# Moving digit work on VectorE behind the maxima: an attention and FFN layer on one Trainium2 core

## The chip, the cores and the metric

The kernel runs on one core of one Trainium2 chip. The metric is the device time of one execution in microseconds. Before the change it is 1046.27 us, the median of three runs (1044.57, 1046.27 and 1047.06).

## The reference

The input is `x` of shape (4, 512, 1024): four sequences of 512 tokens. The layer is causal attention with 16 heads of width 64, a residual with layer norm, then a linear layer with int8 weights, and again a residual with layer norm, all in fp32. Cut to what is computed:

```python
q, k, v = (x @ w.T for w in (w_q, w_k, w_v))          # (4, 512, 16 heads, 64)
q, k = rope(q), rope(k)                                # t * cos + rotate_every_two(t) * sin
scores = where(causal, q @ k^T, -1e9) / sqrt(64)
x = layernorm(x + (softmax(scores) @ v) @ w_out.T)
x = layernorm(x + x @ (weight * scales).T)
```

## The kernel before, in words

**Units and periods.** One unit is one sequence and one pair of heads, so there are 32 units `u`. Units 0 to 15 alternate between sequences 0 and 1, units 16 to 31 between sequences 2 and 3. The loop at L565 does one unit per turn, and one turn is called a period here. Period u holds the scores of unit u, its softmax, the product of probabilities and values of unit u-1 (`attend`, L477), and the projections of later units, which are cut into single matmuls (`tickets`) and drawn from a stream by `take(n)`. In period u the stream delivers products (u+1, 1), (u+1, 2) and (u+2, 0); the second number k is 0 for q, 1 for k and 2 for v.

**Digits.** An fp32 projection is made of three fp32r products. Every operand is held as a high digit h, a low digit l, and a combination d of both: `high_x` and `high_w` run on ScalarE, `low_x`, `diff_x`, `low_w` and `diff_w` on VectorE. `split_w` is `low_w` followed by `diff_w`. `product` (L265) first runs 16 matmuls on h and l into one PSUM buffer, which I call A(u,k), then 8 matmuls on d into a second, D(u,k). ScalarE copies A into `tA` (L292), and VectorE joins D and `tA` (L315). That last step, "the eviction", frees the buffer of D. The pool for these has two buffers, so D(u,k) cannot start before the D ahead of it is evicted.

**Softmax.** `scores` fills three PSUM tiles (groups 0, 1, 2) of a pool with three buffers. `maxima` on VectorE masks and reduces, `softmax` runs exponentials on ScalarE, reciprocals on VectorE and the scaling on GpSimd (L451). Then `transposes` turns the probabilities on VectorE (L456), sends them to DRAM (`turned`) and reads them back as `prT`. `attend` needs a buffer of the pool of score tiles, so it starts only when the exponentials of group 0 have been taken. `turn_values` (L470) turns the values v of a unit on VectorE, sends them to DRAM (`turned_v`) and reads them back as `va`, for `attend` one period later. The tile of v has one buffer (L250), so v of the next unit cannot be evicted before the copy to `turned_v` has read the last one.

**Order.** The order on PE, VectorE and ScalarE is the order of the Python calls. Work outside the loop's own order is hung up with `later(u, slot, f)` and done by `run(u, slot)`; the slots of a period are, in order: early, between, after, first, turn, mid, second, late, end. The order of the DMA issues on SyncE (SP) and of GpSimd's work comes out of the build. Each queue is in order: an instruction that waits holds all that are behind it.

**New sequences.** When unit u+2 belongs to another sequence, `new_sequence` (L321) loads its x in four parts of 512 KB through a ring of three `stage` buffers and hangs up the digit work of the parts. This occurs for u = 14 and 15 (sequences 2 and 3), and for u = 30 and 31, where the "sequences" are the two halves of `w_out` (B and B+1); u = 31 has a list of its own, which the change leaves alone. ScalarE's `high_w(0)` for the first rows of the output product is in slot early of period 30 and waits for a load named `sa`.

Of the kernel before, what the change touches and what calls it, by code (L numbers as in the profile page):

```python
# [38 lines left out]
def attention_ffn_kernel(  # L39
# [107 lines left out]
    def later(u, slot, f):  # L147
        plan.setdefault((u, slot), []).append(f)
# [8 lines left out]
    def load_x2(b, n, tile=None):  # L157


        t = staged[b, n] = stage(f"sx_{b}_{n}", [P, 2, S]) if tile is None else tile  # L160
        cs = slice(2 * n, 2 * n + 2)
        nc.sync.dma_start(out=t, in_=xT[b, :, cs, :] if b < B else wo[:, cs, ts(b - B, S)])
# [5 lines left out]
    def low_x(b, n):  # L168
        h, l, d = (t[:, 2 * n : 2 * n + 2, :] for t in XD[b % 2])
        nc.vector.tensor_tensor(l, staged.pop((b, n)), h, SUB)  # L170
# [5 lines left out]
    def load_w(k, hp):  # L176
        t = staged["w", k] = stage(f"sw_{k}_{hp}", [P, NC, P])
        nc.sync.dma_start(out=t, in_=(wq, wk, wv)[k][hp])

    def load_ao(t, tile=None):  # L180

        tile = staged["w", t % 3] = stage(f"sa_{t}", [P, NC, P]) if tile is None else tile
        nc.sync.dma_start(out=tile, in_=ao[t // NI][:, :, ts(t % NI, P)])
# [25 lines left out]
    def high_w(k):  # L209
        t = staged["w", k]  # L210
        nc.scalar.activation(WD[k][0], t, AF.Copy, scale=LESS)
        nc.scalar.activation(t, t, AF.Copy, scale=1.0 / X12)

    def low_w(k):
        h, l, d = WD[k]
        nc.vector.scalar_tensor_tensor(l, h, -1.0 / X12, staged.pop(("w", k)), op0=MUL, op1=ADD)  # L216

    def diff_w(k):
        h, l, d = WD[k]
        nc.vector.tensor_tensor(d, h, l, SUB)  # L220

    def split_w(k):
        low_w(k)
        diff_w(k)

    with tc.tile_pool(name="raw", bufs=2) as rawp, tc.tile_pool(name="qk", bufs=2) as qkp, ExitStack() as heads:
        def rope(u, k):

            raw, rot = prod.pop((u, k)), prod.pop(("rot", u, k))
            if u not in qk:  # L230
                qk[u] = qkp.tile([P, 2, S], FP, tag="qk", name=f"qk_{u}")
            nc.vector.tensor_mul(rot, rot, sin_sb[:, k, :])  # L232
            nc.vector.tensor_mul(raw, raw, cos_sb[:, k, :])
            out = qk[u][:, k, :]
            if k == 0:

                out = out.rearrange("p (i r s) -> p r i s", i=NI, r=R)
                raw, rot = (t.rearrange("p (r i s) -> p r i s", i=NI, r=R) for t in (raw, rot))
            nc.vector.tensor_add(out, raw, rot)  # L239

        def swap(u, k):

            raw = prod[u, k]
            rot = prod["rot", u, k] = rawp.tile([P, S], FP, tag="rot", name=f"rot_{u}_{k}", bufs=2)
            for p in range(2):
                nc.sync.dma_start(out=rot[p::2, :], in_=raw[1 - p :: 2, :])

        def raw_tile(u, k):
            tag = "v" if k == 2 else "raw"
            t = prod[u, k] = rawp.tile([P, S], FP, tag=tag, name=f"{tag}_{u}_{k}", bufs=1 if k == 2 else 2)  # L250
            return t
# [13 lines left out]
        def product(u, k, n):  # L265

            b, hp = units[u]
            w, r = WD[k], XD[b % 2]
            if n in (0, 2 * NC):
                prod["A" if n == 0 else "D"] = pjp.tile([P, S], FP, tag="pj", name=f"p_{u}_{k}_{n}")  # L270
            ps = prod["A" if n < 2 * NC else "D"]
            c, part = (n // 2, n % 2) if n < 2 * NC else (n - 2 * NC, 2)
            nc.tensor.matmul(  # L273
                ps,
                lhsT=w[part][:, c, :],
                rhs=r[part][:, c, :],
                start=n in (0, 2 * NC),
                stop=n in (2 * NC - 1, NT - 1),
            )
            last = u == NU - 1  # L280
            more = last or units[u + 1][1] != hp

            if more and n == 0:
                load_ao(k) if last else load_w(k, units[u + 1][1])

            b_next = units[u + 2][0] if u + 2 < NU else B + b % 2
            x_next = k == 2 and b_next != b
            if x_next and n == 0:
                new_sequence(u, b_next, True)
            if n == 2 * NC - 1:  # L290
                prod["tA"] = rawp.tile([P, S], FP, tag="tA", name=f"tA_{u}_{k}")
                nc.scalar.activation(prod["tA"], ps, AF.Copy, scale=1.0 + X12)  # L292
                if x_next:
                    new_sequence(u, b_next, False)
                if more:

                    scalar = ("early" if last else None, "first", None)[k]
                    if scalar:
                        later(u - 1, scalar, lambda: high_w(k))
                    else:  # L300
                        high_w(k)
                    vector = ((u - 1, "first"), (u - 1, "late"), (u, "between"))[k]
                    if u == 1:
                        vector = (None, vector, (0, "end"))[k]
                    if last and k != 1:
                        l, d = (((u - 1, "turn"), (u - 1, "mid")), None, ((u, "after"), (u, "after")))[k]
                        later(*l, lambda: low_w(k))
                        if k == 2:

                            later(*l, lambda: low_x(b_next, 0))  # L310
                        later(*d, lambda: diff_w(k))
                    else:
                        later(*vector, lambda: split_w(k))
            if n == NT - 1:
                nc.vector.scalar_tensor_tensor(raw_tile(u, k), ps, -X12, prod["tA"], op0=MUL, op1=ADD)  # L315
                if k < 2:
                    swap(u, k)
                    slot = ("first" if last else "between" if u % 2 else "turn") if k == 0 else "turn"
                    later(u - 1, slot, lambda: rope(u, k))

        def new_sequence(u, b, begin):  # L321


            if b == B + 1:
                if begin:
                    later(u - 1, "mid", lambda: load_x2(b, 0))
            else:
                for n in range(3):
                    (load_x2 if begin else high_x)(b, n)
            if begin:  # L330
                return

            def each(f, *ns):
                return lambda: [f(b, n) for n in ns]

            if b <= B:
                steps = (
                    (u - 1, "late", each(low_x, 0)), (u - 1, "late", each(load_x2, 3)),
                    (u - 1, "late", each(low_x, 1, 2)), (u - 1, "late", each(diff_x, 0, 1)),
                    (u - 1, "end", each(high_x, 3)), (u - 1, "end", each(low_x, 3)),  # L340
                    (u, "late" if b == B else "first", each(diff_x, 2, 3)),
                )
            else:

                steps = (
                    (u - 1, "late", each(load_x2, 1)), (u - 1, "late", each(high_x, 0)),
                    (u - 1, "late", lambda: load_x2(b, 2, qkp.tile([P, 2, S], FP, tag="qk", name="last_2"))),
                    (u, "early", lambda: load_x2(b, 3, qkp.tile([P, 2, S], FP, tag="qk", name="last_3"))),
                    (u, "early", each(high_x, 1, 2)), (u, "first", lambda: more_rows(2)),
                    (u, "first", each(high_x, 3)), (u, "first", each(low_x, 1, 2)),  # L350
                    (u, "second", each(low_x, 3)), (u, "second", lambda: more_rows(3)),
                    (u, "late", each(diff_x, 0, 1, 2, 3)),
                )
            for step in steps:
                later(*step)
# [114 lines left out]
        def turn_values(u):  # L470

            rows = turn(prod.pop((u, 2)), turned["v"])
            va[u] = vap.tile([P, NI, R, Q], FP, tag="va", name=f"va_{u}")
            for a in range(R):
                nc.sync.dma_start(out=va[u][:, :, a, :], in_=rows[:, a, :].rearrange("p (k s) -> p k s", s=Q))
# [20 lines left out]
        with tc.manual_schedule(  # L496
# [56 lines left out]
                whole_product(1, 0)  # L553
                load_w(0, 1)
            later(0, "between", lambda: diff_w(2))
            later(0, "after", lambda: high_w(0))
            later(0, "first", lambda: split_w(0))
            later(0, "late", lambda: (diff_x(0, 3), rope(1, 0)))

            prp, prTp, st1, otp, vap = (  # L560
                heads.enter_context(tc.tile_pool(name=name, bufs=bufs))
                for name, bufs in (("pr", 1), ("prT", 1), ("st", 3), ("ot", 2), ("va", 2))
            )
            turn_values(0)
            for u in range(NU):  # L565
                scores(u)
                run(u, "early")
# [48 lines left out]
    with tc.tile_pool(name="row", bufs=1) as rowp, tc.tile_pool(name="sum", bufs=2) as sump, tc.tile_pool(  # L616
# [54 lines left out]
        with tc.manual_schedule(engines={mybir.EngineType.PE}):  # L671
            for t in range(NT_ROWS):
                early = t + 2
# [68 lines left out]
```

## Time and profile before

| What | Value |
|---|---|
| Median of three runs | 1046.27 us |
| The profiled execution's own time | 1045.79 us |
| Span of that execution | 1044.0 us |
| Busy share of PE, VectorE, ScalarE, GpSimd | 97%, 81%, 37%, 18% |
| Mean granted TensorE clock | 0.991 |
| One steady period (scores at 318.87, next at 340.32) | 21.45 us |

The profile describes one execution. Rows of a timeline give the start, the duration, the engine, the line and the operation; a bracket gives idle time of the engine ahead of the row and what ended it. Rows of the table of waits give the total, the number of times and the longest wait. In a table by stretch, the first number is the length, then come the busy times of the engines with the number of instructions, and at the end the granted clock, the share of the DMA engines and GB/s.

### The profile page before, as it was taken

How to read it: one execution, taken by the hardware profiler on the slowest of the kernel's cores; microseconds unless marked ns; L12 is line 12 of the kernel's file. 1: busy time of each engine (PE TensorE's matmuls, PEld its weight loads, DVE VectorE, ACT ScalarE, POOL GpSimd, SP SyncE). 2: the span in 40 equal slices, each digit the busy share in tenths (PEclk: the TensorE clock that was granted, in tenths of full speed). 3: DMA queues.
4: the chain of work that ended last, by engine and by line, in shares of the span. 5: the costliest groups of instructions: out<-in, count | busy, mean ns of one | idle time of the engine just before them, and what ended most of it. 6: DMA issues, size and time to landing. Idle time of an engine off the chain costs nothing.

```text
span 1044.0 us, 13663 instructions
## 1 busy us (share of the span) xinstructions
PE 1012.8 (97%) x4708; PEld 753.2 (72%) x4708; DVE 844.3 (81%) x1258; ACT 389.3 (37%) x854; POOL 190.6 (18%) x281
## 2 busy tenths in 40 slices
PE   9989999999999989999999999988899999999997
PEld 3557777777777667777777777665688888888885
DVE  5988888988889979798897988888987667767566
ACT  4525354354544335444354353544241121121110
POOL 0112233222322212422223212221100000000000
PEclk9999999999999999999999999999999999999999
DMA  7566765767667876576766767688633222221201
GB/s 281 156 206 196 237 216 196 256 212 217 225 194 250 260 246 206 178 247 215 244 212 197 230 226 225 210 254 262 198 95 121 81 81 81 83 80 60 81 21 60
DMA packets 202453, 190.44 MB, mean 182 GB/s; under 512 B 92688, under 2 KB 158736, under 8 KB 202256
## 3 DMA queue, kind: packets, MB, share of 16 engines
q1 hardware_dynamic: 194896, 172.01, 51.8%
q10 hardware_dynamic: 5328, 9.70, 2.5%
q0 software_dynamic: 2160, 7.87, 1.9%
q8 instruction: 37, 0.61, 0.2%
q14 instruction: 32, 0.26, 0.1%
HBM read 105.64 MB, written 67.11 MB: 165 GB/s over the span
## 4 chain that ended last, share of the span: by engine, by line
PE 68%; issue 9%; DVE 8%; DMA 8%; POOL 3%; SPq 1%; ACT 1%; DVEq 0%; ACTq 0%; POOLq 0%
PE p L273 29%; PE y L196 15%; PE f L646 11%; PE o L483 5%; PE s L406 4%; DMA turned<-pr 3%; POOL pr L451 3%; PE pw L258 2%; DVE pr L456 2%; PE xT L632 1%; DMA turned_v<-v 1%; DVE x_l L170 1%; DMA sx<-in_wo 1%; DVE rot L232 1%; DVE nmx L423 1%
## 5 line engine op out<-in xcount | busy, mean ns | idle before, releaser
L273 PE MATMUL p<-x_h,w_h 128*128 128x512 f32 x736 | 290.5, 395 | 1.0 <-ACT tA L292 1.0
L273 PE MATMUL p<-x_l,w_l 128*128 128x512 f32 x736 | 287.0, 390 | 0.8 <-DVE w_l L216 0.8
L451 POOL TENSOR_SCALAR pr<-pr,rden 128x128 f32<-128x128 f32 (+3 forms) x256 | 179.7, 723 | 554.5 <-DVE rden L445 280.2
L273 PE MATMUL p<-x_d,w_d 128*128 128x512 f32 x736 | 191.1, 395 | 0.6 <-DVE v L315 0.4
L273 PEld LDWEIGHTS p<-x_h,w_h 128*128 128x128 f32 x736 | 138.1, 188 | 53.5 <-issue 23.5
L437 ACT ACTIVATE pr<-s,nmx 128x128 f32<-128x128 f32 (+3 forms) x256 | 131.6, 531 | 106.6 <-DVE nmx L423 106.6
L273 PEld LDWEIGHTS p<-x_d,w_d 128*128 128x128 f32 x736 | 135.5, 188 | 34.4 <-issue 5.3
L273 PEld LDWEIGHTS p<-x_l,w_l 128*128 128x128 f32 x736 | 138.2, 188 | 29.3 <-DVE w_l L216 1.3
L292 ACT ACTIVATE tA<-p 128x512 f32<-128x512 f32 x92 | 55.2, 600 | 220.2 <-PE p L273 214.4
L456 DVE STREAM_TRANSPOSE pr<-pr 128x768 f32<-128x768 f32 (+1 forms) x96 | 99.6, 1054 | 19.8 <-POOL pr L451 19.7
L196 PE MATMUL y<-x_h,w_h 128*128 128x512 f32 x256 | 102.6, 401 | 4.7 <-DVE row L205 3.9
L423 DVE TENSOR_REDUCE nmx<-s 128x2 f32<-128x256 f32 (+3 forms) x128 | 102.5, 821 | 3.4
L196 PE MATMUL y<-x_l,w_l 128*128 128x512 f32 x256 | 101.1, 395 | 0.2 <-DVE w_l L216 0.2
L646 PE MATMUL f<-wf,x1hi 128*128 128x512 f32 x240 | 93.6, 390 | 0.0
L646 PE MATMUL f<-wf,x1lo 128*128 128x512 f32 x240 | 93.5, 389 | 0.0
L483 PE MATMUL o<-prT,va 128*64 128x256 f32 (+3 forms) x512 | 81.0, 461 | 12.5 <-ACT pr L437 12.5
L315 DVE SCALAR_TENSOR_TENSOR raw<-p,tA 128x512 f32<-128x512 f32 x61 | 41.7, 684 | 50.3 <-PE p L273 50.3
L483 PEld LDWEIGHTS o<-prT,va 128*64 128x64 f32 x512 | 35.5, 142 | 61.8 <-issue 42.3
L406 PE MATMUL s<-qk 64*128 64x384 f32 (+3 forms) x512 | 77.7, 443 | 1.0 <-DVE qk L239 1.0
L220 DVE TENSOR_TENSOR w_d<-w_h,w_l 128x1024 fp32r<-128x1024 f32 x60 | 74.2, 1237 | 1.5
L196 PE MATMUL y<-x_d,w_d 128*128 128x512 f32 x256 | 64.3, 392 | 0.9 <-DVE sin_sb L205 0.5
L196 PEld LDWEIGHTS y<-x_h,w_h 128*128 128x128 f32 x256 | 48.6, 190 | 16.2 <-DVE row L205 4.3
(103 smaller groups left out, 1167.4 us busy)
## 6 DMA issues: line engine op xcount, KB each, us to landing
turned<-pr SPq DMA_DIRECT2D x64, 384.0 KB, 3.1
rot<-raw SPq DMA_DIRECT2D x128, 128.0 KB, 2.1
turned<-pr SPq DMA_DIRECT2D x32, 512.0 KB, 4.5
prT<-turned SPq DMA_DIRECT2D x32, 512.0 KB, 4.9
prT<-turned SPq DMA_DIRECT2D x32, 384.0 KB, 4.0
turned_v<-v SPq DMA_DIRECT2D x32, 256.0 KB, 3.8
va<-turned_v SPq DMA_DIRECT2D x128, 64.0 KB, 2.6
prT<-turned SPq DMA_DIRECT2D x32, 256.0 KB, 3.4
```

Source lines behind the costliest of these rows:

```text
L196: nc.tensor.matmul(ps, lhsT=r[part][:, c, :], rhs=w[part][:, c, :], start=n in (0, 2 * NC), stop=n in (2 * NC - 1, NT - 1),)
L220: nc.vector.tensor_tensor(d, h, l, SUB)
L273: nc.tensor.matmul(ps, lhsT=w[part][:, c, :], rhs=r[part][:, c, :], start=n in (0, 2 * NC), stop=n in (2 * NC - 1, NT - 1),)
L292: nc.scalar.activation(prod["tA"], ps, AF.Copy, scale=1.0 + X12)
L315: nc.vector.scalar_tensor_tensor(raw_tile(u, k), ps, -X12, prod["tA"], op0=MUL, op1=ADD)
L406: nc.tensor.matmul(ps[:, j, at : at + n], lhsT=t[rows, 0, ts(i, P)], rhs=keys[rows, :, : (i + 1) * Q], start=True, stop=True,)
L423: nc.vector.tensor_reduce(nmx[:, 2 * i : 2 * i + 2], ps[:, :, at : at + n], AX.X, ALU.max, negate=True)
L437: nc.scalar.activation(pr[:, :, at // P : at // P + i + 1, j, :], ps[:, j, at : at + n].rearrange("p (r k s) -> p r k s", r=R, s=Q), AF.Ex ...
L451: nc.gpsimd.tensor_scalar(p, p, rden[:, m : m + 1], 1.0, ALU.mult, ALU.mult)
L456: nc.vector.transpose(t, t)
L483: nc.tensor.matmul(ps[j * D : (j + 1) * D, kb * P :], lhsT=v[:, kb, 2 * j : 2 * j + 2, :].rearrange("p a s -> p (a s)"), rhs=t[:, :, 4 * k ...
L646: nc.tensor.matmul(ps, lhsT=part[:, c, :], rhs=wfv[:, c, o], start=(c == 0 and part is hi), stop=(c == NC - 1 and part is lo),)
```

## The change

Three lists of work are put in another order; no arithmetic is added or removed.

1. At a change of sequences (u = 14, 15 and 30), VectorE's `low_x` of part 3 and `diff_x` of parts 0 and 1 leave the end of period u-1 for slot between of period u, behind the maxima and the first two groups of softmax.
2. In period 0, `turn_values(0)` leaves the place ahead of the loop for slot first. `high_w(0)` on ScalarE goes from slot after to slot early, and `split_w(0)` on VectorE from first to after.
3. `split_w(2)` of the second pair of heads goes from slot end of period 0 to slot between of period 1.

```diff
@@ product @@
                     if u == 1:
-                        vector = (None, vector, (0, "end"))[k]
+                        vector = (None, vector, (1, "between"))[k]
@@ new_sequence @@
-                    (u - 1, "late", each(low_x, 1, 2)), (u - 1, "late", each(diff_x, 0, 1)),
-                    (u - 1, "end", each(high_x, 3)), (u - 1, "end", each(low_x, 3)),
+                    (u - 1, "late", each(low_x, 1, 2)), (u - 1, "end", each(high_x, 3)),
+                    (u, "between", each(low_x, 3)), (u, "between", each(diff_x, 0, 1)),
                     (u, "late" if b == B else "first", each(diff_x, 2, 3)),
@@ ahead of the loop over periods @@
-            later(0, "after", lambda: high_w(0))
-            later(0, "first", lambda: split_w(0))
+            later(0, "early", lambda: high_w(0))
+            later(0, "after", lambda: split_w(0))
+            later(0, "first", lambda: turn_values(0))
             later(0, "late", lambda: (diff_x(0, 3), rope(1, 0)))
@@ after the pools are opened @@
-            turn_values(0)
             for u in range(NU):
```

SyncE's order follows: the copy `turned_v` of unit 0 with the four reads of `va` moves from ahead of all copies of probabilities to behind the third of them; the next load of `w_q` moves ahead of them; and at a change of sequences the copies of v go ahead of one or two of the loads.

## The prediction

> **What bounds it now.** PE is busy 97% of the span, so I asked first who makes PE wait (table of waits of PE; columns: total, times, longest):
>
> ```profile
> PE o L483 <- ACT pr L437: 12.5, 5, 3.3
> PE s L406 <- DVE qk L239: 1.0, 1, 1.0
> PE p L273 <- ACT tA L292: 1.0, 1, 1.0
> PE p L273 <- DVE w_l L216: 0.8, 1, 0.8
> ```
>
> Five waits of `attend` make up 12.5 us. PE's timeline shows where they and the other waits lie:
>
> ```profile
> 42.76 0.50 PE L273 MATMUL p<-x_h,w_h 128*128 128x512 f32 x1 [1.00 <-ACT tA L292]
> 49.97 0.50 PE L273 MATMUL p<-x_l,w_l 128*128 128x512 f32 x1 [0.81 <-DVE w_l L216]
> 56.91 2.43 PE L406 MATMUL s<-qk 64*128 64x128 f32 x16 [1.05 <-DVE qk L239]
> 66.56 3.98 PE L483 MATMUL o<-prT,va 128*64 128x512 f32 x16 [2.90 <-ACT pr L437]
> ...
> 348.71 2.37 PE L483 MATMUL o<-prT,va 128*64 128x512 f32 x16 [1.64 <-ACT pr L437]
> 373.15 4.06 PE L483 MATMUL o<-prT,va 128*64 128x512 f32 x16 [2.90 <-ACT pr L437]
> 388.30 2.11 PE L273 MATMUL p<-x_d,w_d 128*128 128x512 f32 x8 [0.43 <-DVE v L315]
> ...
> 701.10 4.07 PE L483 MATMUL o<-prT,va 128*64 128x512 f32 x16 [3.32 <-ACT pr L437]
> ```
>
> These are periods 0 and 1, 14 and 15, and 30: the places that the change touches. Between them PE has no wait at all. The release is always the exponentials, but VectorE's timeline shows that these were late because digit work stood ahead of the maxima:
>
> ```profile
> 340.11 2.35 DVE L174 SCALAR_TENSOR_TENSOR x_d<-x_l,x_h 128x1024 fp32r<-128x1024 f32 x2
> ...
> 343.67 1.23 DVE L170 TENSOR_TENSOR x_l<-sx,x_h 128x1024 fp32r<-128x1024 f32 x1
> 344.81 0.90 DVE L420 TENSOR_TENSOR s<-s,mask 128x256 f32<-128x256 f32 x2
> ```
>
> **The clock rule.** The same `attend` takes 2.37 us at 348.71 and about 4.0 behind the longer waits. By stretch:
>
> ```profile
> 66.50:70.50 4.00, 3.94 (x17) 1.56 (x17) 2.31 (x5) 2.96 (x10) 2.78 (x7) 0.58 0.02 5
> 348.70:351.10 2.40, 2.39 (x17) 1.15 (x17) 2.37 (x5) 2.40 (x8) 1.23 (x2) 1.00 0.38 105
> ```
>
> The granted clock (third number from the end) is 0.58 after 2.90 us of waiting, 1.00 after 1.64. The Trainium skill ("TensorE: Matmul & The Clock Gate", What's actually happening) has the clock fall to half only after a full idle window of about 3.4 us. By it, removing a 2.90 us wait is worth 2.90; by the row, 2.90 + 1.6 (3.98 or 4.06 less 2.37). I take the row: three such rows agree. Over the waits of 2.90 in periods 1 and 15 the two differ by 3.3 us.
>
> **Part 1, change of sequences (periods 14, 15).** What moves is one `low_x` and two `diff_x`, 1.14 + 2.27 = 3.4 us of VectorE per change. Period 14 afterwards: the three `low_x` end at 340.1, v's transpose (0.63) and the eviction (0.60) at 341.3, the scores' first group is there, and the maxima start 3.4 us earlier than 344.81. ScalarE's `high_x(3)` at 342.58 to 343.6 is still ahead of the exponentials and just does not hold them: 343.6 instead of 346.94. `attend` was ready at 347.07 and finds its buffer at 345.4: the 1.64 us go. The moved 3.4 us now lie behind the second reciprocal, with the 2.1 us of rope, and delay the last reciprocal; it comes at 352.1, where it was at 351.99. From there VectorE is as late as before: transposes, x_d of parts 2 and 3, rope, eviction of v at 359.9 to 360.5. D(16,0), at 361.59 before, wants to start at 359.95 and needs that eviction: a new wait of 0.6. Net 1.0.
>
> Period 15: low_x to 363.9, transpose, eviction, maxima at 365.1 instead of 369.31. The last part of x can only be loaded behind `low_x(0)` (361.7, was 362.55; 4.0 us to land), so `high_x(3)` ends at 366.7 and does not hold the exponentials (367.2). `attend`'s buffer comes at 368.95; it is ready at 370.25 - 1.0 = 369.2. So 2.90 and the clock's 1.69 go: 5.6 in all. Then VectorE is the bound: from the maxima's end at 369.9, 3.6 us of digits and reciprocals, transposes and eviction to 377.2, x_d to 379.5, two ropes to 383.3, v's eviction to 384.0. D(17,0) wants to start at 387.87 - 5.6 = 382.3 and waits until 384.0, against 388.30: **4.3 us gained**.
>
> *What speaks against it.* The Trainium skill ("GPSIMD Engine Reference", Specifications) says GpSimd shares its SBUF interfaces with VectorE and contends with VectorE's instructions that have two SBUF inputs. The moved ones have two, and stand beside GpSimd's scaling. This trace agrees: its eight instructions take 4.10 us beside a mostly idle VectorE (374.37) and 6.17 beside w_l and w_d (324.91), where the transpose behind them waits 1.11. By the unhindered row I charge nothing, by the hindered one up to 1.1 per period. In period 14 rope behind the digits covers it; in period 15 3.6 us of VectorE's work cover most: 0.3. So **4.0**, between 2.5 and 5.
>
> **Part 2, period 0.** Without the v transpose (0.62) the maxima start at 36.6, exponentials at 38.8. `high_w(0)`, 2.2 us, fits ScalarE's idle 4.55 us ahead of them if w_q, issued at 28.58, has landed (6.3 us for the slowest such load: 34.9). The tA wait falls from 1.00 to 0.4. `split_w(0)` (2.35) now stands ahead of the transposes and of raw(1,1)'s eviction, which goes from 46.6 to 47.5: D(1,2) waits 1.6 us, was 46.69, starts 47.5. In return w_l is ready for A(2,0): the 0.81 goes. The next step is v(1,2)'s eviction. VectorE reaches it at 52.4 (was 53.02). But v has one buffer, so it waits for `turned_v` of unit 0, which is now issued only after v's transpose (50.3) and, in SP's order, behind a probability read that waits for its copy to land (3.1 us as before: 51.9): issue at about 52.5. Its landing is shown only under other loads; SP's rows of `turned_v` and of the read that waits for it:
>
> ```profile
> 343.11 0.33 SPq L457 DMA_DIRECT2D turned_v<-v  x1
> ...
> 349.00 2.58 SPq L475 DMA_DIRECT2D va<-turned_v  x4
> ```
>
> That is 5.9 us with the DMA engines full; 2.1 in the quiet at 37.31; 3.4 at 367.71. Here two large copies are in flight, but the w_q load has gone ahead: I take 3.3, so the eviction starts at V = 55.9. Behind V stand, in VectorE's order: eviction, x_d, rope (scores at V + 3.9), split_w(1), v, eviction, and the maxima of unit 1.
>
> **Part 3, period 1.** Taking `split_w(2)` (2.38 us) out puts the maxima at V + 7.3 and `attend`'s buffer at V + 11.2 (from the rows: 62.67 - 2.38 - 53.02, and 66.56 - 62.67). PE is ready at V + 10.6, so its wait is 0.5 and the clock stays up: `attend` ends at V + 13.5, before at 66.56 + 3.98 = 70.5. Gain = 57.0 - V. The ends: V = 52.4 gives +4.6, V = 58.4 (5.9 us) gives -1.4, V = 55.9 gives **1.1**. w_l of k = 2 is ready long before A(2,2). If D(2,0)'s wait (53.1 to V + 0.6, 3 us) halves the clock, the 1.3 us lie in the wait of the scores for rope. VectorE idled 3.09 us later in period 1, which absorbs its lag.
>
> **Part 1 again, period 30.** The maxima end early as in period 14, but ScalarE has `high_w(0)` ahead of the exponentials:
>
> ```profile
> 697.29 1.06 ACT L211 ACTIVATE w_h<-sa 128x1024 fp32r<-128x1024 f32 x1 [2.27 <-DMA sa<-ao]
> ```
>
> It ended 699.34, and the exponentials started then. So the gain here is what the `sa` load lands earlier. The second `sa` load (512 KB) went beside it and now goes behind the v copies; at 303 GB/s that is 0 to 1.7 us. I take 1.2: `attend` still waits 2.1, the clock stays up, and VectorE's chain (last reciprocal, transposes, w_l) sets the rest: **1.2**.
>
> **Sum.** 4.0 + 1.1 + 1.2 = 6.3 us. Against the profiled execution: 1045.79 - 6.3 = 1039.5, and that execution lay 0.5 below the median: **1040.0**.
>
> **Rivals.**
> (a) Everything clears: v's copy lands by 52.4 (+4.6), `sa` early enough that the clock cost goes too (3.3), 4.3: 12.2 us, 1034.1. Against it: the busy DMA engines at 50 to 56. 0.15.
> (b) Only periods 14 and 15 pay: V at 57 and `sa` as late as before, 4.0: 1042.3. For it: three loads of 512 KB fill the queue at 690. 0.25.
> (c) No measurable change: the waits are handed on in 14 and 15 as well, since VectorE does the same work and each eviction of v comes as late as before, within 1 us: 1045.8. Against it: VectorE idled 1.66 + 1.72 us in period 15. 0.08.
> (d) Slower, by the one buffer of v: every us of V beyond 57.0 is lost outright. With 5.2 from the others, the time exceeds the old one by 0.2% from V = 64.3, a landing of 11.7 us: 1048.5. No row nears it. 0.06, also for what a queue's order can do that I can't see.
> The likeliest has 0.46, with its own range 1038 to 1042.
>
> **Chances and range.** 0.2% (2.1 us) is about what this kernel's runs can tell from no change. Faster: 0.46 + 0.15 + 0.25 = 0.86; same 0.08; slower 0.06. The range reaches from (a) to just past (b): 1034.5 to 1044.5.
>
> **What would show it.** PE's waits at `attend` near 348 and 370 gone and clock 1.00 there; a new wait on v (L315) of 1 to 2 us at the end of period 15; in period 0 a VectorE wait on the DMA `turned_v` ahead of v's eviction near 52, about 3 us. If that is absent, I am too pessimistic; if D(16,0) waits over 2 us, Part 1 is wrong.

## The result: slower by 0.4%, and the profile after

The changed kernel takes 1049.99 us (median of 20 runs, 1046.75 to 1052.96) against 1045.81 us (20 runs, 1042.52 to 1049.41) for the kernel before: ratio 1.0038, 95% interval 1.0026 to 1.0049. The prediction was 1040.0 us with a range of 1034.5 to 1044.5, so it had the wrong sign. The profiled execution is the fastest of the 20 (1046.75 us, span 1045.0), so it shows less of the loss than the median has.

PE's table of waits in the profile after (total, times, longest), to be read beside the one of before:

```profile
PE o L483 <- ACT pr L437: 6.7, 2, 4.0
PE p L273 <- DVE x_d L174: 4.9, 1, 4.9
PE p L273 <- DVE v L315: 3.9, 2, 2.9
```

Three of the five `attend` waits are gone, as predicted: 12.5 us became 6.7. (The fifth, in period 31, is not listed in the prediction: it was 1.71 us and is 2.64 now.) In their place stand 4.9 us for `x_d` and 3.9 us for v. PE's timeline after shows where:

```profile
45.93 2.11 PE L273 MATMUL p<-x_d,w_d 128*128 128x512 f32 x8 [0.69 <-ACT tA L292]
52.35 1.65 PE L273 MATMUL p<-x_d,w_d 128*128 128x512 f32 x6 [0.69 <-ACT tA L292]
58.85 1.22 PE L273 MATMUL p<-x_d,w_d 128*128 128x512 f32 x2 [4.85 <-DVE x_d L174]
60.88 4.52 PE L406 MATMUL s<-qk 64*128 64x128 f32 x16 [0.80 <-DVE qk L239]
...
348.43 2.37 PE L483 MATMUL o<-prT,va 128*64 128x512 f32 x16
362.39 2.14 PE L273 MATMUL p<-x_d,w_d 128*128 128x512 f32 x8 [0.94 <-DVE v L315]
371.16 2.37 PE L483 MATMUL o<-prT,va 128*64 128x512 f32 x16
387.13 2.11 PE L273 MATMUL p<-x_d,w_d 128*128 128x512 f32 x8 [2.95 <-DVE v L315]
...
700.20 3.96 PE L483 MATMUL o<-prT,va 128*64 128x512 f32 x16 [4.02 <-ACT pr L437]
```

At 348.43 and 371.16 `attend` runs without a wait and at full clock. But D(2,0) stops for 4.85 us after six of its eight matmuls (58.85), the scores behind it take 4.52 us where they took 2.43, D(17,0) waits 2.95 us for v's eviction, and in period 30 the wait grew from 3.32 to 4.02 us.

The start of each unit's scores on PE is a fixed mark in every trace. Its shift against the trace of before, taken as a difference from mark to mark, says where the time went. "Second profile" is of another execution of the same kernel (after_again, below):

| Stretch | Predicted | Profile after | Second profile |
|---|---|---|---|
| Start to scores of unit 2 (82.96 before) | -1.1 | +1.4 | +2.0 |
| Unit 2 to 14 | 0 | 0 | +0.9 |
| Change of sequences, unit 14 to 16 (340.32, 390.34) | -4.0 | -2.6 | -0.7 |
| Unit 16 to 31, with period 30 (719.18) | -1.2 | +0.5 | +2.5 |
| Unit 31 to the end of the span | 0 | +1.6 | +0.8 |
| Sum | -6.3 | +1.0 | +5.5 |

The medians' +4.2 us lies between the two profiles. So the start costs instead of gaining, the change of sequences gains less than forecast, and period 30 costs. Two executions of one kernel differ by 4.5 us here, so a shift read from a single profile says where time went in that execution, and the times of many runs have to say how much it is.

What VectorE does at the start after the change:

```profile
49.30 0.67 DVE L456 STREAM_TRANSPOSE v<-v 128x512 f32<-128x512 f32 x1
...
56.98 0.69 DVE L315 SCALAR_TENSOR_TENSOR v<-p,tA 128x512 f32<-128x512 f32 x1 [5.07 <-DMA turned_v<-v]
57.59 1.21 DVE L174 SCALAR_TENSOR_TENSOR x_d<-x_l,x_h 128x1024 fp32r<-128x1024 f32 x1
```

And SyncE's issue of the copy:

```profile
51.86 0.89 SPq L457 DMA_DIRECT2D turned_v<-v  x1
```

The predicted wait on `turned_v` is there, ahead of v's eviction, but it is 5.07 us long and not about 3. The copy is issued at 51.86 and its buffer comes free at 56.98. `x_d` of part 3, which D(2,0) needs, stands right behind it at 57.59.

### The profile page after: what moved, and what is told of

It is laid out like the page before. It is cut to its first block, busy times and chain, and to the rows that moved or that the text cites. A ratio compares the mean times of both kernels' runs of the same rounds, so it can differ in the third digit from the quotient of the medians.

```text
span 1045.0 us, 13666 instructions
## 1 busy us (share of the span) xinstructions
PE 1012.7 (97%) x4708; PEld 754.6 (72%) x4708; DVE 844.3 (81%) x1258; ACT 389.5 (37%) x854; POOL 203.0 (19%) x281
## 4 chain that ended last, share of the span: by engine, by line
PE 81%; DVE 7%; DMA 5%; issue 4%; POOL 1%; ACT 1%; SPq 0%; DVEq 0%; ACTq 0%; POOLq 0%
PE p L273 40%; PE y L196 15%; PE f L646 11%; PE s L406 6%; PE o L483 6%; POOL pr L451 1%; DVE x_d L174 1%; PE xT L632 1%; DVE x_l L170 1%; DVE pr L456 1%; DMA turned<-pr 1%; ACT pr L437 1%; DMA sx<-in_xT 1%; DMA sa<-ao 1%; PE pw L258 1%
## 5 line engine op out<-in xcount | busy, mean ns | idle before, releaser
L451 POOL TENSOR_SCALAR pr<-pr,rden 128x128 f32<-128x128 f32 (+3 forms) x256 | 192.5, 771 | 541.6 <-DVE rden L445 281.6
L483 PE MATMUL o<-prT,va 128*64 128x256 f32 (+3 forms) x512 | 77.6, 446 | 6.7 <-ACT pr L437 6.7
L406 PE MATMUL s<-qk 64*128 64x384 f32 (+3 forms) x512 | 79.8, 452 | 0.8 <-DVE qk L239 0.8
## 6 DMA issues: line engine op xcount, KB each, us to landing
turned<-pr SPq DMA_DIRECT2D x64, 384.0 KB, 3.2
prT<-turned SPq DMA_DIRECT2D x32, 384.0 KB, 4.1
```

The lines of the kernel that those rows point to most:

```text
L406: nc.tensor.matmul(ps[:, j, at : at + n], lhsT=t[rows, 0, ts(i, P)], rhs=keys[rows, :, : (i + 1) * Q], start=True, stop=True,)
L451: nc.gpsimd.tensor_scalar(p, p, rden[:, m : m + 1], 1.0, ALU.mult, ALU.mult)
L483: nc.tensor.matmul(ps[j * D : (j + 1) * D, kb * P :], lhsT=v[:, kb, 2 * j : 2 * j + 2, :].rearrange("p a s -> p (a s)"), rhs=t[:, :, 4 * k ...
```

## The experiments

Theory of the loss at the start: the late copy holds v's eviction, and what costs is what is queued behind it. Theory at the change of sequences: the digits stand at a bad place, behind reciprocals that wait for ScalarE. The rivals were that other edits cost the time (`split_w` late), or that VectorE is the bound of periods 14 and 15 wherever the digits stand. In what follows, "unit 2", "unit 16" and "unit 31" are the shifts of these scores against before, in us and from one profile each. All runs but the last one (clock_probe) are in one table; the ratio is to runs of the kernel before on the same chip, and it is not the quotient of two medians:

| Kernel | Median, us | Ratio (95%) | Unit 2 | Unit 16 | Unit 31 |
|---|---|---|---|---|---|
| after_again | 1050.15 | 1.0025 (1.0015 to 1.0035) | +2.0 | +2.2 | +4.7 |
| start_only | 1049.70 | 1.0025 (1.0015 to 1.0035) | +2.1 | +2.8 | +2.5 |
| tv_only | 1048.61 | 1.0016 (1.0007 to 1.0026) | +0.8 | +0.2 | +0.1 |
| seq_only | 1046.73 | 1.0004 (0.9992 to 1.0016) | +0.1 | +1.5 | +2.0 |
| after_xd | 1046.63 | 0.9998 (0.9987 to 1.0008) | -2.3 | -2.9 | -2.8 |
| seq_bank | 1045.62 | 0.9982 (0.9970 to 0.9993) | -0.7 | -1.8 | +1.2 |
| seq_slot | 1044.58 | 0.9973 (0.9961 to 0.9985) | +0.2 | -3.6 | -3.6 |
| v_ahead | 1044.45 | 0.9966 (0.9955 to 0.9977) | -4.3 | -3.2 | -3.3 |
| start_v_ahead | 1044.01 | 0.9972 (0.9962 to 0.9981) | -3.8 | -4.5 | -5.0 |
| v_slot | 1042.81 | 0.9958 (0.9944 to 0.9973) | -3.8 | -8.1 | -6.9 |
| best1 | 1039.61 | 0.9928 (0.9913 to 0.9944) | -3.0 | -5.6 | -8.1 |

### The changed kernel once more, and each half alone

after_again has no edit. seq_only is the kernel before with the lines of `new_sequence` changed alone (periods 14, 15 and 30); start_only is the kernel before with the edits of the start alone (`turn_values(0)`, `high_w(0)`, `split_w(0)` and `split_w(2)` moved).

> The changed kernel once more. The first trace of it (1046.75 us) is the fastest of its twenty runs, whose median is 1049.99. Theory W (waits): the loss is the 5.07 us in which VectorE waits for the copy of v in period 0, with half the clock behind it, the same in every run; then this trace should again end about 1 us later than the one of before, and the rest of the median is unexplained. Theory C (clock): several new waits of PE lie at 2.6 to 4.9 us (D(2,0) 4.85, D(17,0) 2.95, attend in period 30 4.02 and in 31 2.64), and whether the clock falls behind the shorter ones changes from run to run; then a run at 1050 shows half the clock behind a wait of 2.6 to 3.0 where the first trace shows full clock. Median 1049 to 1051.

> Only the change of sequences (part 1) put on the kernel before; the start of the kernel is as before. If the loss is all from the start, this is faster than before by 2 to 4 us (the two traces show 2.6 us gained between the scores of units 14 and 16): 1042 to 1044. If the new waits at D(17,0) (about 3 us) and in period 30 (4 us) cost the clock, it is slower than before: 1047 to 1049, with half the clock behind one of these.

> Only the start (turn_values(0), high_w(0), split_w(0), split_w(2) moved), with the change of sequences as before. If the loss is all from the start: slower than before by 1.5 us (attend of period 1 ended 1.45 us later in the first trace of the changed kernel) to 4 us: 1047.5 to 1050. If the loss comes from the change of sequences: within 1.5 us of before.

The loss of the changed kernel is there again (ratio 1.0025). start_only has all of it (1.0025), seq_only is level with before. So the start costs, and the moved digits bring nothing that these runs can tell, where 4.0 us had been forecast for the change of sequences and 1.2 for period 30.

The granted clock, which is on record for every run, says in what form the start costs. Time lost to the clock is (1 - granted clock) times the span. Its mean is 12.4 us in the 22 runs of after_again and 12.6 in those of start_only, against 9.9 in the 71 runs of before beside them: 2.5 and 2.7 us more. The mean times differ by 2.7 us in both cases. So what the clock takes is about as large as the whole loss.

### v ahead: the start without the late copy

v_ahead is the changed kernel with one line put back; start_v_ahead leaves the digits where they were as well.

```diff
-            later(0, "first", lambda: turn_values(0))
...
+            turn_values(0)
             for u in range(NU):
```

> The changed kernel with turn_values(0) put back ahead of the loop, everything else kept. The copy of v is then issued near 37 us and nothing waits for it. If the single buffer of v is what costs at the start, VectorE reaches v's eviction at about 52.5, attend of period 1 waits 0.5 us at full clock and ends near 66, 4.6 us earlier than before, and the time is 4 to 8 us under before: 1038 to 1042. If split_w(0) ahead of the transposes or the change of sequences costs, it stays at 1046 or above.

> The kernel before with only the start's high_w(0), split_w(0) and split_w(2) moved; turn_values(0) stays ahead of the loop and the change of sequences is as before. Theory (the start gains 57.0 - V with V = 52.4, so 4.3 to 4.6, and the moved digits lose 1 us at the change): unit 2's scores 4.3 us earlier than 82.96, unit 16's still 3.5 to 4.3 us earlier, where the version that also moves the digits had 3.2; 1041.5 to 1043.5. Rival (the digits gain when the start is not late): 1045 or more.

With the copy early, VectorE's timeline of start_v_ahead has no wait ahead of v's eviction:

```profile
52.48 0.68 DVE L315 SCALAR_TENSOR_TENSOR v<-p,tA 128x512 f32<-128x512 f32 x1
```

V is 52.48, and unit 2's scores come 3.8 us earlier (4.3 in v_ahead), where the prediction's formula, 57.0 - V, gives 4.5. One line of the change turns a loss into a gain of 0.3%, and the mean loss to the clock falls to 7.9 us in v_ahead and 8.0 in start_v_ahead. Between the two kernels the moved digits make no difference that these runs can tell; in the traces they lose 1.1 us between unit 14 and 16 in v_ahead.

### The late copy alone, and the work behind the eviction

tv_only is the kernel before with `turn_values(0)` in slot first. after_xd is the changed kernel with the late copy kept, and only the two things behind it moved ahead of the eviction:

```diff
-            later(0, "late", lambda: (diff_x(0, 3), rope(1, 0)))
+            later(0, "second", lambda: (diff_x(0, 3), rope(1, 0)))
```

> The kernel before with one edit: turn_values(0) in slot first of period 0, behind split_w(0). Theory (the single buffer of v, read behind the late copy turned_v, is what costs at the start): v's eviction starts at about 57 instead of 53.0, D(2,0) then waits 3 to 5 us on x_d of part 3, and the scores of unit 2 start 1 to 4 us later than at 82.96; 1048 to 1051. Rival (the other edits of period 0 cost it: split_w(0) and split_w(2) late): this kernel is level with the one before or up to 1 us faster, 1045.5 to 1047.

> The changed kernel with one edit: diff_x(0, 3) and rope(1, 0) in slot second of period 0 instead of late, that is ahead of v(1,2)'s eviction on VectorE and not behind it. The copy turned_v stays as late as in the changed kernel. Theory (what costs is what stands behind the waiting eviction, above all x_d of part 3, and the clock that PE loses while it waits 4.85 us for it): v's eviction still starts at about 57, but D(2,0) does not wait, the scores of unit 1 start at about 56, as in the version with v ahead (56.4), and those of unit 2 1.5 to 3.1 us earlier than in the kernel before (82.96), where the changed kernel has them 1.43 later; 1045.5 to 1047.5. Rival (the late eviction itself costs, through the maxima of unit 1 and attend(0)): unit 2 no earlier than in the kernel before, 1049 or more.

tv_only is slower by 0.16% on its own: the eviction starts at 55.39 and D(2,0) waits 2.60 us for `x_d`. That is less than expected (V about 57, a wait of 3 to 5 us), but the direction is the theory's. after_xd shows the rest. Its VectorE timeline:

```profile
52.24 1.22 DVE L174 SCALAR_TENSOR_TENSOR x_d<-x_l,x_h 128x1024 fp32r<-128x1024 f32 x1
54.70 0.69 DVE L239 TENSOR_TENSOR qk<-raw,rot 128x512 f32<-128x512 f32 x1
57.42 0.69 DVE L315 SCALAR_TENSOR_TENSOR v<-p,tA 128x512 f32<-128x512 f32 x1 [2.03 <-DMA turned_v<-v]
```

The eviction is as late as in the changed kernel (57.42), yet D(2,0) runs through, the scores of unit 1 start at 55.54, and unit 2's come 2.3 us earlier than before instead of 1.4 later. So it was not the late eviction that cost the 3.8 us between these two, but `x_d` and rope queued behind it (which of the two was not taken apart). In time after_xd is level with before (0.9998); its profile is the fastest of its 14 runs, so the 2.3 us are not the gain of its median. A second buffer for v would take the wait itself away; no run here has one.

### Where the digits stand

seq_slot is the kernel before with the same digits moved, but to a place right behind the three maxima, ahead of the softmax calls and so of the first reciprocals. Against seq_only:

```diff
-                    (u, "between", each(low_x, 3)), (u, "between", each(diff_x, 0, 1)),
+                    (u, "maxed", each(low_x, 3)), (u, "maxed", each(diff_x, 0, 1)),
...
                 for g in range(3):
                     maxima(u, g)
+                run(u, "maxed")
                 softmax(u, 0)
                 softmax(u, 1)
                 run(u, "between")
```

> The kernel before with the digits of the change of sequences (low_x of part 3, diff_x of parts 0 and 1) run right behind the three maxima, ahead of softmax and so ahead of both reciprocals. Theory (where they were moved to, they stand behind reciprocals that wait for exponentials held by high_x(3), so VectorE idles and its chain gets late): the digits fill that idle time, no wait of VectorE on pr of 0.9 us in periods 14 and 15, the scores of unit 16 start 2 to 4 us earlier than before (390.34); 1043 to 1045. Rival (the work is merely handed on, VectorE is the bound of period 15 wherever the digits stand): unit 16 within 1.5 us of before, 1046 to 1048.

It gains 0.27% where the change's own place gains nothing (not all of that is the place, as the next section shows). VectorE's timeline of seq_only shows what is wrong with slot between:

```profile
347.36 0.18 DVE L445 RECIPROCAL rden<-den 128x4 f32<-128x4 f32 x1 [0.86 <-ACT pr L437]
348.48 0.17 DVE L445 RECIPROCAL rden<-den 128x2 f32<-128x2 f32 x1 [0.95 <-ACT pr L437]
348.56 1.31 DVE L170 TENSOR_TENSOR x_l<-sx,x_h 128x1024 fp32r<-128x1024 f32 x1
```

VectorE is through with the maxima and stands still for 1.8 us with 3.4 us of digit work behind the reciprocals. They wait for exponentials, which stand on ScalarE behind `high_x(3)`, which waits for the load of the last part of x. From issue to the start of `high_x(3)` that took 4.5 us in the kernel before, 4.8 in the profile after, 5.4 in after_again, 5.6 in seq_only and 6.0 in v_ahead. Everything behind in VectorE's queue is late, and PE's timeline of seq_only shows who waits:

```profile
356.44 2.11 PE L273 MATMUL p<-x_d,w_d 128*128 128x512 f32 x8 [1.43 <-DVE raw L315]
363.57 2.14 PE L273 MATMUL p<-x_d,w_d 128*128 128x512 f32 x8 [1.40 <-DVE v L315]
...
388.21 3.68 PE L273 MATMUL p<-x_d,w_d 128*128 128x512 f32 x8 [2.87 <-DVE v L315]
```

The gain of `attend` (two waits, 4.54 us, and the clock) comes back as three waits of 5.7 us, the last with the clock's loss (3.68 us for 2.11). In seq_slot PE's timeline has two of them, 2.2 us, with the last one on another releaser:

```profile
362.06 2.11 PE L273 MATMUL p<-x_d,w_d 128*128 128x512 f32 x8 [1.48 <-DVE v L315]
384.71 2.11 PE L273 MATMUL p<-x_d,w_d 128*128 128x512 f32 x8 [0.69 <-ACT tA L292]
```

### A bank of PSUM

That last row asked for one more run. v's eviction in period 15 starts at 386.41 in seq_slot and at 386.39 in the changed kernel, and yet D(17,0) starts at 384.71 in the one and at 387.13 in the other. So D(17,0) can't have used the bank of D(16,2), which holds v until this eviction: in seq_slot the build had put it into the bank of A(17,0), in the changed kernel and in seq_only into that of D(16,2). seq_bank is seq_only with this one bank exchanged by naming the two banks; the order on every engine is the same.

```diff
+    turn_of = [0]
+
+    def bank(own=False):
+        turn_of[0] += not own
+        return f"pj{turn_of[0] % 2}"
...
-                prod["A" if n == 0 else "D"] = pjp.tile([P, S], FP, tag="pj", name=f"p_{u}_{k}_{n}")
+                prod["A" if n == 0 else "D"] = pjp.tile([P, S], FP, tag=bank((u, k) == (17, 0) and n > 0), name=f"p_{u}_{k}_{n}")
```

> The version with the digits of the change of sequences alone moved to slot between, with one more edit: D(17,0) gets the PSUM bank of A(17,0) and not that of D(16,2), by naming the two banks; every other product keeps its bank, and the order on every engine is the same. Theory (the digits' move makes v's eviction of period 15 no later than before, but the build's choice of bank ties D(17,0) to it, and that wait of 2.9 us, with or without the clock's 1.7, eats what attend gained): D(17,0) waits 0.7 us for tA, the scores of unit 16 start at about 388.1, 2.2 us ahead of before's 390.34 and 2.0 to 3.7 ahead of the version without this edit (391.83); 1043 to 1045. Rival (VectorE's chain is the bound of period 15 whatever the bank, through rope for the scores of unit 16): unit 16 within 1 us of 391.8 less the clock's 1.7, and the time within 1 us of that version's, 1046 to 1047.

PE's timeline of seq_bank (lines are 6 higher there):

```profile
386.49 2.11 PE L279 MATMUL p<-x_d,w_d 128*128 128x512 f32 x8 [0.69 <-ACT tA L298]
388.53 2.43 PE L412 MATMUL s<-qk 64*128 64x128 f32 x16
```

D(17,0) runs from 386.49, while v's eviction only starts at 388.06. The scores of unit 16 start 3.3 us earlier than in seq_only, of which the clock has 1.7. The ratio goes from 1.0004 to 0.9982, with intervals that touch at 0.9992 and 0.9993, and the time is 0.6 us above what was expected. The trace says more clearly than the times that the wait of 2.9 us belonged to the bank.

This leaves the place of the digits with less than seq_slot seemed to give it. seq_slot differs from seq_only in place and bank together, and so do v_slot and best1 below, where D(17,0) also waits 0.69 us for `tA`. With the old bank D(17,0) could not have started in seq_slot before 387.1, the end of v's eviction, and it started 2.4 us earlier: that much of its 3.8 us between units 14 and 16 is the bank's, by this estimate. In time, the old place with the good bank (0.9982) and the new place with it (0.9973) have overlapping intervals. The new place with the old bank has no run.

### The clock by itself

clock_probe is the kernel before with VectorE made late in eleven periods of the steady stretches, so that `attend` waits a chosen time. Its time of 1097.2 us means nothing.

```diff
+        LATE = {3: 8, 5: 9, 7: 10, 9: 11, 11: 12, 17: 8, 19: 9, 21: 10, 23: 11, 25: 12, 27: 13}
...
+                for n in range(LATE.get(u, 0)):
+                    nc.vector.tensor_reduce(
+                        stats[u][0][:, :2], s_ps[u, 0][:, :, GROUPS[0][0][1] : GROUPS[0][0][1] + (GROUPS[0][0][0] + 1) * P], AX.X, ALU.max, negate=True
+                    )
                 for g in range(3):
                     maxima(u, g)
```

> The kernel before with VectorE made late on purpose in eleven periods of the steady stretches: the first maximum of group 0 is taken 8, 9, 10, 11 and 12 times more in periods 3, 5, 7, 9 and 11, and 8 to 13 times more in periods 17, 19, 21, 23, 25 and 27 (the same result each time, 0.5 us each). Attend waits in each of these periods; with 2.0 us of slack the waits are about 2.0, 2.5, 3.0, 3.5, 4.0 and once more, to 4.5. Measured is for each wait whether the granted clock falls to a half behind it and what the next stretch costs. Theory (the row's reading, a fixed threshold between 1.7 and 2.9 us): all waits from 2.9 on halve the clock for about 4 us, none under 2 does. Rival (a window that runs free of the wait): waits of the same length between about 1.7 and 3.4 us halve it in one place and not in another, and from 3.4 on all do; a wait of 2.9 us is then worth 1.6 us more only in some executions.

PE's timeline of clock_probe:

```profile
112.73 2.38 PE L484 MATMUL o<-prT,va 128*64 128x512 f32 x16 [1.79 <-ACT pr L438]
158.30 4.06 PE L484 MATMUL o<-prT,va 128*64 128x512 f32 x16 [2.25 <-ACT pr L438]
...
678.39 4.54 PE L484 MATMUL o<-prT,va 128*64 128x512 f32 x16 [4.08 <-ACT pr L438]
```

Both waits of 1.79 us (the second ends at 440.56) keep the clock, and all nine from 2.25 us on in this series lose it. That alone speaks for a fixed threshold. But the same wait of D(17,0) does not fit one: 2.95 us in the profile after and 2.91 in after_again kept the clock, 2.87 in seq_only, 2.92 in after_xd and 2.96 in v_ahead lost it. So the rival, a window that runs free of the wait, has the better of it, and the traces show the window. In each of them the stretches at half clock begin on a grid of 3.413 us. Cut at this grid, seq_only (first two rows) and the profile after (last three) look like this at the wait of D(17,0); PE's busy time is the second number:

```profile
384.87:388.28 3.41, 0.54 (x4) 0.12 (x2) 3.31 (x7) 2.60 (x3) 0.00 (x0) 1.00 0.84 257
388.28:391.69 3.41, 3.41 (x8) 2.37 (x8) 0.62 (x1) 0.00 (x0) 0.00 (x0) 0.50 0.67 224
...
382.59:386.00 3.41, 1.60 (x8) 0.98 (x6) 3.34 (x7) 1.74 (x3) 0.00 (x0) 1.00 0.96 312
386.00:389.41 3.41, 2.28 (x12) 1.66 (x14) 1.84 (x4) 0.86 (x1) 0.00 (x0) 1.00 0.61 183
389.41:392.82 3.41, 3.41 (x22) 2.13 (x21) 3.20 (x7) 0.54 (x3) 0.00 (x0) 1.00 0.34 121
```

In seq_only the wait falls whole into one window, and the next window has half the clock. In the profile after a line of the grid, at 386.00, cuts the wait into 1.81 and 1.13 us, and the clock stays. The last section has the count over all traces. The probe could not show this by itself: its series repeats every 47.8 us, which is 14 windows, and each of its nine losing waits had 2.25 us or more inside one window.

### Taken together

v_slot has the start of v_ahead and the digits right behind the maxima. best1 moves in addition ScalarE's `high_w(0)` of period 30 from early to between, so that the exponentials do not stand behind the load `sa`:

```diff
-                    scalar = ("early" if last else None, "first", None)[k]
+                    scalar = ("between" if last else None, "first", None)[k]
```

> The early start of the version with v ahead, the digits right behind the maxima, and in period 30 high_w(0) on ScalarE in slot between instead of early, so that the exponentials do not wait for the load sa. Theory: 4.3 from the start, 2 to 4 at the change of sequences, 0 to 3 in period 30: 1036 to 1041. Rival (what is gained ahead of period 30 is swallowed by the loads of w_out, which land when they land): 1043 or more, with the wait on row at 742.7 moved by less than 1 us.

> The last version without its third edit: v ahead of the loop and the digits right behind the maxima, with high_w(0) of the output product back in slot early of period 30. Theory (start and change of sequences pay, period 30's load sa decides the rest): unit 16 scores 5.5 us earlier than before, as with that third edit; unit 31 only 4.5 to 5.5 earlier against 8.1; and the time within 1.5 us of 1039.6, since the wait on row in period 31 takes what period 30 gained. Rival (the third edit was worth its 3 us at the end as well): 1042 to 1043.

best1 is faster than both kernels: 1039.61 us, 0.7% below before. v_slot came 3.2 us above it, outside the 1.5 expected, so the rival held there: the edit in period 30 seems worth its time at the end as well, with intervals that touch (six runs each). PE's timeline of best1 shows what is left:

```profile
716.85 0.50 PE L196 MATMUL y<-x_h,w_h 128*128 128x512 f32 x1 [3.36 <-DVE cos_sb L205]
```

Unit 31 starts 8.1 us earlier than before, but the span is only 4.9 us shorter: in period 31 the loads for the output product are not earlier by as much. PE waits here until VectorE has added a product to a row of x (its tile is that of `cos_sb`). VectorE waits for that row to land and starts at 716.10, 5.6 us earlier than before, and ScalarE's first conversion from a tile `last` of `w_out` starts 5.7 us earlier.

## Why the prediction was wrong

**Part 2, period 0 (V = 55.9): wrong in the landing, and in what stands behind it.** The landing of `turned_v` was taken as 3.3 us, between the shown 2.1 and 5.9; it took 5.1 (51.86 to 56.98). With V = 56.98 the formula gives a gain of 0.0, where 1.1 had been forecast. That is the smaller half. The larger is the step that D(2,0)'s stop hides: "the 1.3 us lie in the wait of the scores for rope". The scores did start where the formula has them, at V + 3.9 (60.88). But the stop is at `x_d` and not at v's eviction, it is 4.85 us long, and the half clock behind it reaches past the wait for rope. Windows of the profile after on the clock's grid, with the granted clock third from the end:

```profile
54.91:58.32 3.41, 0.00 (x0) 0.00 (x0) 1.34 (x2) 0.00 (x0) 0.00 (x0) 1.00 0.84 272
58.32:61.73 3.41, 2.07 (x8) 1.39 (x10) 3.38 (x5) 0.00 (x0) 0.00 (x0) 0.50 0.52 87
61.73:65.14 3.41, 3.41 (x12) 1.54 (x10) 3.34 (x6) 0.00 (x0) 0.00 (x0) 0.50 0.57 195
```

The clock stayed at half from 58.32 to 65.14, through the scores, which took 2.1 us more with no cover. PE was ready for `attend` at 69.6 and not at V + 10.6 = 67.6. The start came out 1.4 us late at unit 2 and 2.0 in the second profile. after_xd shows that this was the price of the order behind the eviction. The formula itself was good where the clock stays up: V = 52.48 gave 3.8 where it says 4.5.

**The prediction's rivals.** Rival (d), slower, had the place (the one buffer of v) but not the mechanism. It counted what V loses beyond 57.0, with a gain of 5.2 elsewhere, and set the turn at V = 64.3. V was 56.98, so by its own count the start would have lost nothing; the loss is the clock's behind D(2,0), and the gains elsewhere did not come. Rival (c), waits handed on in periods 14 and 15 because each eviction of v comes as late as before, is close to what seq_only shows: v's eviction of period 15 starts at 387.48 there, and at 387.56 before. It had a chance of 0.08.

**Part 1, change of sequences: the waits went as forecast, the gain did not.** Both `attend` waits vanished with the clock's loss. In period 14 the steps hold in the profile after (v's eviction at 361.65, forecast 359.9 plus the 1.4 by which this profile was late; D(16,0) waits 0.94, forecast 0.6). They hold only while the load of the last part lands in 4.8 us. The step that failed is "`high_x(3)` at 342.58 to 343.6 is still ahead of the exponentials and just does not hold them": it had no margin, and from a landing of 5.4 us on VectorE idles behind it. after_again then gains 0.7 us between units 14 and 16 and seq_only loses 1.4. I had moved the loads along with VectorE's work, but not asked what their new neighbours on the queues do to them. (The four traces with these loads in their old place have 4.4 to 4.6 us, the nine with the loads moved 4.6 to 6.0; which neighbour delays them is not shown.)

In period 15 v's eviction was forecast to end at 384.0 and D(17,0) to wait 1.7 us. VectorE's timeline after:

```profile
372.26 0.17 DVE L445 RECIPROCAL rden<-den 128x2 f32<-128x2 f32 x1 [0.44 <-ACT pr L437]
...
376.67 0.98 DVE L456 STREAM_TRANSPOSE pr<-pr 128x768 f32<-128x768 f32 x1 [0.68 <-POOL pr L451]
...
386.39 0.68 DVE L315 SCALAR_TENSOR_TENSOR v<-p,tA 128x512 f32<-128x512 f32 x1
```

It ends at 387.07, 3.1 us behind the forecast: 1.0 is the shift that this profile has at unit 15, 0.8 a later start of the maxima (366.86 against 365.1 and that shift), 0.44 the wait for the exponentials, 0.68 the wait for GpSimd; 0.2 is left over. And I took it as given that D(17,0) needs this eviction. The statement ahead of the prediction that D(u,k) cannot start before the D ahead of it is evicted is wrong: which buffer a product gets was the build's choice, which I had treated as a fixed rotation. seq_bank and seq_slot show it at D(17,0), and the profile after at the start: D(1,2) was to wait for raw(1,1)'s eviction until 47.5 and began at 45.93, and D(2,0) began at 52.35, ahead of v's eviction at 56.98.

**The contention with GpSimd was undercharged.** Its eight scaling instructions took 8.50 and 7.18 us beside the moved digits, 5.46 and 4.10 before, and 5.50 and 4.11 in seq_slot, where the digits are done before scaling begins. I charged 0 and 0.3 us. What of it reached VectorE in period 15 is the 0.68 above; rope's product with the cosines, beside it in period 14, took 0.88 us, where it had 0.77 before and 0.68 with GpSimd idle.

**Part 1 again, period 30: wrong sign.** The `sa` load was issued 2.4 us earlier, but ScalarE's digits follow by less. SyncE's row before, the one after, and ScalarE's after:

```profile
690.58 1.36 SPq L183 DMA_DIRECT2D sa<-ao  x2
...
688.18 0.56 SPq L183 DMA_DIRECT2D sa<-ao  x1
...
696.40 1.06 ACT L211 ACTIVATE w_h<-sa 128x1024 fp32r<-128x1024 f32 x1 [1.98 <-DMA sa<-ao]
```

The digits were at 697.29 before. From issue to this row it is 8.2 us where it was 6.7, so of the 2.4 us only 0.9 are left, less than the 1.6 by which unit 30 itself was early. The wait of `attend` grew to 4.02 us instead of shrinking to 2.1. I had read it as relief that the second `sa` load "now goes behind the v copies". In the trace after, the copy of v is issued at 689.93, beside the first `sa` load; that it delayed the load is likely and not shown. In period 31 the first conversion from a tile `last` of `w_out` starts at 725.72 against 725.80, and the 0.7 us still in hand at unit 31 are gone. The rest of the +1.6 us at the end goes with the clock: PE waits 3.88 us for VectorE at a row of x in both profiles (until 742.80 before, 742.71 after), and two windows at half clock go with that wait after the change, where it was one before.

**The clock.** The prediction took 1.6 us for every wait of 2.90 us or more, from three rows that agree. Three rows could not show that a wait of this length sometimes keeps the clock (2.95 in the profile after), and the costly case was left out: a stop with two windows at half clock behind it.

**Right:** where `attend` waits and why, the wait of v's eviction on `turned_v`, new waits on v at the ends of periods 14 and 15, and that their size decides.

## What to carry to other kernels

A wait that is removed from one engine is worth only what the next in-order queue leaves of it: before moving work, write down what stands right behind every instruction that will wait, and move the urgent part (here `x_d` and rope) ahead of it. Put work that is to fill a gap in front of the instruction that waits, not behind it: behind the reciprocals the digits left VectorE idle for 1.8 us and gained nothing, ahead of them there was no such wait, and together with another bank they gained 0.27%. And treat a buffer that the build assigns, and the landing time of a load whose neighbours change, as unknowns with a price, not as the row of before.

## What the runs showed of the hardware

**The clock is decided window by window.** In each of the fourteen traces the stretches at half clock begin at multiples of 3.413 us from one another, to within 2 ns, and last one or two such windows, once three (leaving out the end of a trace). One window at half clock is 1.7 us lost, two are 3.4. I cut PE's work behind the first 30 us of every trace at this grid. Of 4069 windows at full clock, 70 had 1.97 us or more of idle time on PE, and half the clock followed each of them; the other 3999 had 1.84 us at most, and it followed none. Of 77 windows at half clock, the 16 with 0.75 us of idle time or more were followed by another, the 61 with 0.60 us at most were not. So what counts is not the length of a wait but how much of it falls into one window.

By length alone it looks like chance. Over thirteen of the fourteen traces (all but seq_bank) I took every PE wait of 1 us or more behind the first 30 us. None of 28 waits below 1.8 us lost anything, 20 of 28 between 1.97 and 2.97 us did, and 38 of 39 from 3.0 us on; the one exception, 3.60 us in clock_probe, was cut by the grid into 1.77 and 1.84.

The Trainium skill ("TensorE: Matmul & The Clock Gate", What's actually happening) describes a free-running activity window of about 3.4 us, and half of it is an estimate of 1.7 us for one window, which the grid and the loss per window match. The traces do not match its condition of an idle window as long as that: here 1.97 us of idle time inside one window were enough. For a forecast, the place of the grid is not known beforehand. A wait of 2 to 3 us is worth its length plus about 0.7 times 1.7 us, with 20 of 28 for the factor, and a longer one its length plus 1.7 or 3.4.

**Landing times move.** The same 256 KB copy `turned_v` took 4.8 to 5.3 us in the kernels that issue it late, where the kernel before had 2.1 in the quiet of the start, and the same 512 KB load of x took 4.4 to 6.0 us from issue to its first use, from kernel to kernel, and 4.8 and 5.4 us in two executions of the changed one. Both swings are larger than the 1.1 and 1.2 us that had been forecast for the start and for period 30.
